# Where the spread reciprocals of the fourth pair are loaded in layer 0, and where the last pair's reciprocal is taken in layer 1

## The chip, the cores and the metric

The kernel runs on one core of one Trainium2 chip. The metric is the time of one execution on the device in microseconds (us), the median of several runs; lower is better. The core's engines are TensorE (PE, matrix products), VectorE (DVE), ScalarE (ACT), GpSimd (POOL) and SyncE (SP). SP issues nearly all transfers (DMA); ACT issues a few in layer 0. Each engine works through its own instructions in the order of the program and waits where an operand isn't there yet.

## The reference, cut to what matters

Eight images of 384 channels and 32 x 32 pixels pass through two layers. Layer 0 is attention over the 1024 pixels with 8 heads of 48 channels and a bias per pair of positions; layer 1 is attention with 6 heads of 64 channels and normalised q and k, and then a feed-forward part. What the change touches is, in both layers, the division of the attention's output by the sums of its exponentials, and what is done with the quotient:

```python
# layer 0
attn = jnp.einsum('bhnd,bhmd->bhnm', q * scale, k)
attn = attn + _relative_bias(h, w, mlp_w1, mlp_b1, mlp_w2, mlp_b2)[None]
attn = jax.nn.softmax(attn, axis=-1)
out = jnp.einsum('bhnm,bhmd->bhnd', attn, v)
out = out.transpose(0, 2, 1, 3).reshape(b, n, c)
out = out @ proj_w + proj_b
# layer 1
attn = jax.nn.softmax(jnp.einsum('bhnd,bhmd->bhnm', q, k) * scale, axis=-1)
out = jnp.einsum('bhnm,bhmd->bhnd', attn, v)
out = out.transpose(0, 2, 1, 3).reshape(B, N, C)
return out @ proj_w.T + proj_b
```

The kernel computes exp(scores) and its product with v first, takes the sums of the exponentials along as an extra row of that product, and divides afterwards.

## The kernel before, in words

**Layout.** The eight heads of layer 0 are handled as four pairs (numbers 0 to 3; the name NF0 is 3). A pair's two heads lie in the two halves of 64 partitions (S0 = 64) of a tile of 128 x 1024. A head needs only 48 of its 64 partitions, so the fourth pair's rows are also laid into the spare partitions of the other three: the output projection then has three products over the pairs in place of four. `oT` holds the attention's output of all four pairs; row 0 of each half of a pair is the sum of the exponentials.

**The boundary between two images in layer 0.** While PE finishes image b, the next image's queries and keys are projected, in six blocks n = 0 to 5 (keys and queries of the first pair, then of the second and third). A block's products come out of PE; `take` (line 677, ACT) copies the smaller part to a tile `t`; `add` (line 683, DVE) adds the larger part; `halves` splits the result: ACT makes the rounded high half `h` (line 696) and issues its stores (lines 701 and 703, tensor `halves` in memory), DVE makes the low half by subtraction (line 697), and SP issues its stores (the same two lines). The fourth pair's rows of q and k sit in the other pairs' tiles, so for the first pair the operands are put together on the chip by transfers from tile to tile (`move`, line 719): two for the queries' last operand, at once; two in `fill_q`; and eight in `fill_k`, the tiles called `h`, `l` and `km` in the profile.

**The division of a pair** (`divide`, line 947 on): two transfers bring the row of sums to memory (`sd`); `invert` reads them back in another shape and POOL raises them to the power -1 (line 961); `keep_inverse` stores the reciprocals (`rd`, line 967); `spread` loads them twice, each time broadcast over 64 partitions (`rb`, two transfers of 256 KB, line 984); `multiply` multiplies `oT` by them on POOL (line 988); for the fourth pair `spread_rows` copies its rows into the spare partitions of the other pairs' `oT` (six transfers, line 1000). Then comes the output projection of image b, `pp` (line 1011).

**What sets the order.** The order is written out by hand. `_Later.after(n, work)` puts work down for the n-th next call of `step()`, and `step()` is called at fixed places of the program, for example at the end of each `add` (line 683). The tuple `at` in `divide` holds four such numbers: the steps from the division to `keep_inverse`, from the division to `spread`, from `spread` to `multiply`, and from `multiply` to `spread_rows`. Images 0 to 6 use the tuple that the change touches for the fourth pair. After that pair's division the steps of the boundary are, in order: add of n=0, add of n=1, add of n=2, the four parts `project_v(0)` to `project_v(3)` of the values' projection, add of n=3, add of n=4, add of n=5. In the code `fill_q` follows `project_v(1)`, `fill_k` follows `project_v(2)`; each part of the projection ends with a step. The held `halves` of block n=3 come ahead of the add of n=4. All of SP's transfers are issued in this order, and a transfer that must wait holds back those behind it.

The tiles of q, k, `t` and `h` come from one pool of slots; a slot is handed on when its last reader is done.

**Layer 1.** Images 1 to 4 take the first block of the next image's q and k between the attention of image b and its output projection. `project_cut` (line 1775 on) runs the products, ACT copies one part (line 1791), and its inner function `take` evicts: DVE combines both parts (line 1800) and ACT squares the result (line 1802). With `step=False` it returns `take` to the caller in place of running it and stepping. `divide` of layer 1 (line 1996 on) puts the sums in memory and reads them back to `inv`; its `invert` takes the reciprocal on DVE (line 2024), stores it (line 2026) and loads it spread over the partitions (`rb`, two transfers, line 2033); `multiply` (line 2042, DVE) follows a step later, between the two parts of `project_out` (line 2076, `pp`).

Of the kernel before, what the change touches and what calls it, by code (L numbers as in the profile page):

```python
# [200 lines left out]
class _Weights:  # L201
# [32 lines left out]
    def take(self):  # L234
        for at, n, pm in self.sums:
            self.nc.vector.tensor_scalar_mul(self.mean[:, at : at + n], pm[:, :n], 1.0 / C)
# [39 lines left out]
def _layer0(tc, ins, x1, sums, shared, weights, beside):  # L276
# [9 lines left out]
    with ExitStack() as ctx:  # L286
# [14 lines left out]
        later = _Later()  # L301
# [25 lines left out]
        for g in range(P // QT):  # L327
            at = g * QN
# [618 lines left out]
        def divide(b, pair):  # L947


            o = oT[:, pair]  # L950
            sd = dram.tile([2, N], F32, tag="sd", name=f"sd{b}_{pair}")
            rd = dram.tile([2, N], F32, tag="rd", name=f"rd{b}_{pair}")
            mine = sums[:, b, pair]
            inv = kept.tile([P, 2 * N // P], F32, tag="inv", name=f"inv{b}_{pair}", bufs=2)
            for j in range(2):
                nc.sync.dma_start(sd[j : j + 1], oT[j * S0 : j * S0 + 1, pair])

            def invert():
                with nc.allow_non_contiguous_dma(reason="sums"):
                    nc.sync.dma_start(mine, sd.rearrange("j (p c) -> (j p) c", c=2 * N // P))  # L960
                    nc.gpsimd.tensor_tensor(  # L961
                        inv, mine, over.to_broadcast([P, 2 * N // P]), ALU.pow
                    )

            def keep_inverse():
                with nc.allow_non_contiguous_dma(reason="sums"):
                    nc.sync.dma_start(rd.rearrange("j (p c) -> (j p) c", c=2 * N // P), inv)

            if b == B - 1 or b == 0 and pair < NF0:
                invert()  # L970
                at = (2, 2 if pair == NF0 else 3, 2, 0)
            elif pair == NF0:
                invert()
                at = 2, 5, 2, 1
            else:
                later.after(1, invert)
                at = 3, 4, 2, 0
            later.after(at[0], keep_inverse)
            rb = []

            def spread():
                rb.append(kept.tile([P, N], F32, tag="rb", name=f"rb{b}_{pair}"))
                for j in range(2):
                    nc.sync.dma_start(rb[0][ts(j, S0)], rd[j].partition_broadcast(S0))
                later.after(at[2], multiply)

            def multiply():
                nc.gpsimd.tensor_mul(o, o, rb[0])  # L988
                if b == B - 1:
                    if pair < NF0:  # L990
                        for j in range(2):
                            nc.gpsimd.memset(oT[j * S0 : j * S0 + SP, pair], 0.0)
                elif pair == NF0:
                    later.after(at[3], spread_rows)

            def spread_rows():
                for c in range(NF0):
                    for j in range(2):
                        row = j * S0 + SP + c * FR
                        nc.sync.dma_start(oT[j * S0 : j * S0 + SP, c], oT[row : row + FR, pair])  # L1000

            later.after(at[1], spread)
# [70 lines left out]
        for i in range(len(parts) // 2):  # L1073
            later.after(i + (13 if i < 9 else 12), lambda: grow_turns(1))
            at = 1 + i % NF0 if i < 12 else 2 + i % 2
# [480 lines left out]
def _layer1(tc, ins, x1, out, shared, start, there, before=None, check=None):  # L1556
# [4 lines left out]
    with ExitStack() as ctx:  # L1561
# [10 lines left out]
        later = _Later()  # L1572
# [138 lines left out]
        def project_qk(b, pair, s, xt, dst, sq, step=True, middle=None):  # L1711


            pq = mm2(f"pq{b}_{pair}_{s}")
            order = [(k, h) for k in range(KC) for h in range(NH)]
            for k, h in order if middle is None else sorted(order, key=lambda kh: kh[1]):
                if middle is not None and (k, h) == (0, 1):
                    middle()
                nc.tensor.matmul(  # L1719
                    pq[:, h], wqkv[:, k, s * C + pair * P : s * C + (pair + 1) * P],  # L1720
                    xt[:, k, ts(h, HALF)], start=(k == 0), stop=(k == KC - 1),
                )

            def take():
                t = qkp.tile([P, N], F32, tag="qk", name=f"qk{b}_{pair}_{s}")
                if s == 0:
                    nc.vector.tensor_copy(t, flat2(pq))
                else:
                    nc.vector.tensor_copy(
                        t.rearrange("c (m p) -> c p m", m=MT),  # L1730
                        flat2(pq).rearrange("c (p m) -> c p m", m=MT),
                    )
                dst[pair, s] = t
                q = wtile(f"qsq{b}_{pair}_{s}")
                nc.scalar.activation(q, flat2(pq), AF.Square)
                sq[pair, s] = q

            if not step:
                return take
            take()  # L1740
            later.step()
# [37 lines left out]
        def project_cut(b, n, parts, dst, sq, step=True, middle=None, order=(2, 0, 1)):  # L1779


            pair, s = BLOCKS1[n]
            name = f"{b}_{pair}_{s}"
            ps = mm2("pg" + name), mm2("pm" + name)
            for at, i in enumerate(order):
                if middle is not None and at == 2:
                    middle()
                cuts.products(n, i, ps[i // 2], (parts.high, parts.low, parts.mixed)[i])

            q = wtile("qsq" + name)  # L1790
            nc.scalar.activation(q, flat2(ps[1]), AF.Identity, scale=-1.0 / CUT)

            def take():
                t = qkp.tile([P, N], F32, tag="qk", name="qk" + name)
                to = t if s == 0 else t.rearrange("c (m p) -> c p m", m=MT)
                of = flat2(ps[0])
                if s == 1:
                    of = of.rearrange("c (p m) -> c p m", m=MT)
                with_ = q if s == 0 else q.rearrange("c (p m) -> c p m", m=MT)
                nc.vector.scalar_tensor_tensor(to, of, 1.0 + 1.0 / CUT, with_, ALU.mult, ALU.add)  # L1800
                dst[pair, s] = t
                nc.scalar.activation(with_, to, AF.Square)
                sq[pair, s] = q

            if not step:
                return take
            take()
            later.step()
# [53 lines left out]
        def project_v(b, xt, m2, c=None, copy=nc.vector.tensor_copy):  # L1862

            pv = mm2(f"pv{b}_{m2}")
            for i in range(2):
                for k in range(KC):
                    nc.tensor.matmul(  # L1867
                        pv[:, i, 0:C],
                        xt[:, k].rearrange("c (p m) -> c m p", m=MT)[:, 2 * m2 + i],
                        wv[:, k], start=(k == 0), stop=(k == KC - 1),  # L1870
                    )
            if c is None:
                copy(v[:, 2 * m2 : 2 * m2 + 2], pv[:, :, 0:C])
            else:
                for i in range(2):
                    m = 2 * m2 + i
                    nc.vector.tensor_scalar_mul(v[:, m], pv[:, i, 0:C], c[:, 1, m : m + 1])
            later.step()
# [113 lines left out]
        def weigh_last(b, oT, done):  # L1992
            for finish in weigh(b, oT, *done) or ():
                finish()
# [328 lines left out]
        for b in range(B):  # L2323
# [65 lines left out]
            else:  # L2389
                nqk, sq, d, nkc = {}, {}, head_rows(b + 1), kc_tile(b + 1)  # L2390

                def project(n, step=True, middle=None, order=(2, 0, 1)):
                    if b == 0:
                        return project_qk(b + 1, *BLOCKS[n], ahead, nqk, sq, step, middle)
                    return project_cut(b + 1, n, parts, nqk, sq, step, middle, order)
# [4 lines left out]
                if b == 0:  # L2400
                    for i in range(2):
                        project_v(b + 1, ahead, i)
                        weigh_last(b, oT, held[i])
                    divide(b, oT, [NP1 - 1], (1, 1))
                    project_v(b + 1, ahead, 2)
                else:
                    project_v(b + 1, ahead, 0)
                    weigh_last(b, oT, held[0])
                    for k in range(1, KC):
                        parts.cut_low(k)  # L2410
                    weigh_last(b, oT, held[1])
                    divide(b, oT, [NP1 - 1], (1, 1))
                    for k in range(KC):
                        parts.mix(k)
                    project(0, order=(0, 1, 2))
                fsq, fc = [], []
                project_out(b, oT, xt, lambda m, _: fsq.append(square(f"f{b}", xt, m)), later.step)
                if b > 0:
# [14 lines left out]
                if b == 0:  # L2433
                    project(1)
                    take = project(2, step=False)
# [4 lines left out]
                    take = project(3, step=False)  # L2440
# [137 lines left out]
```

## Time and profile before

| | us |
|---|---|
| median of three runs | 2915.94 |
| lowest and highest | 2912.86, 2917.39 |
| the profiled execution, its own time | 2915.22 |
| its span (first to last instruction) | 2913.4 |
| PE busy | 2872.4 (99% of the span) |
| DVE busy | 2010.5 (69%) |
| ACT busy | 1554.4 (53%) |
| POOL busy | 492.7 (17%) |

The mean granted clock of PE over the span is 0.998 of full speed, and 86% of the chain that ended last lies on PE. Layer 0 lasts to about 1340 us; the seven boundaries between its images lie about 162 us apart, the first at some 230 us.

How to read the rows: in a row of the waits, "PE s L920 <- DMA l<-h: 10.3, 6, 1.8" says that PE, ahead of the instructions of line 920 that write `s`, waited in total 10.3 us, 6 times, 1.8 at most, for a transfer that writes `l` from `h`. "SPq" is SP's queue. In a timeline each row has the start in us from the span's start, the length, the engine, the line and operation, out<-in by the program's names, the number of instructions, and in brackets the idle time just before with what ended it. Loads of weights into PE (PEld) run beside its products.

### The profile page before, as it was taken

How to read it: one execution, taken by the hardware profiler on the slowest of the kernel's cores; microseconds unless marked ns; L12 is line 12 of the kernel's file. 1: busy time of each engine (PE TensorE's matmuls, PEld its weight loads, DVE VectorE, ACT ScalarE, POOL GpSimd, SP SyncE). 2: the span in 40 equal slices, each digit the busy share in tenths (PEclk: the TensorE clock that was granted, in tenths of full speed). 3: DMA queues.
4: the chain of work that ended last, by engine and by line, in shares of the span. 5: the costliest groups of instructions: out<-in, count | busy, mean ns of one | idle time of the engine just before them, and what ended most of it. 6: DMA issues, size and time to landing. Idle time of an engine off the chain costs nothing.

```text
span 2913.4 us, 43519 instructions
## 1 busy us (share of the span) xinstructions
PE 2872.4 (99%) x16850; PEld 1648.2 (57%) x16850; DVE 2010.5 (69%) x2041; ACT 1554.4 (53%) x1888; POOL 492.7 (17%) x318
## 2 busy tenths in 40 slices
PE   8999999999999999999999999999999999999998
PEld 3465564646464554644546647647647647655553
DVE  3886868686777768673756865865865875865756
ACT  2655636364555647362734655555555555564644
POOL 3120302121120202022102203203202202211010
PEclk9999999999999999999999999999999999999999
DMA  6657575665746474753301212112112112112111
GB/s 193 198 166 207 136 237 136 192 173 167 193 139 194 131 233 99 225 142 109 110 24 31 84 32 73 68 32 72 68 32 72 68 32 73 68 41 84 41 46 39
DMA packets 177751, 324.78 MB, mean 111 GB/s; under 512 B 75744, under 2 KB 94672, under 8 KB 176256
## 3 DMA queue, kind: packets, MB, share of 16 engines
q1 hardware_dynamic: 167552, 299.88, 36.1%
q10 hardware_dynamic: 9984, 22.02, 2.4%
q8 instruction: 137, 2.24, 0.3%
q14 instruction: 78, 0.64, 0.1%
HBM read 227.50 MB, written 80.65 MB: 106 GB/s over the span
## 4 chain that ended last, share of the span: by engine, by line
PE 86%; DMA 4%; DVE 4%; ACT 2%; issue 1%; SPq 1%; ACTq 0%; POOL 0%; DVEq 0%
PE o L893 14%; PE s L1930 11%; PE o L1979 11%; PE s L920 11%; PE y2p L2224 6%; PE pg L171 6%; PE y1p L2173 5%; PE pv L1867 4%; PE pm L171 3%; PE pp L2076 3%; PE pp L1011 3%; PE vg L776 2%; PE pq L1719 2%; PE s L824 1%; PE o L855 1%
## 5 line engine op out<-in xcount | busy, mean ns | idle before, releaser
L931 ACT ACTIVATE e<-e 128x1024 f32<-128x1024 f32 x448 | 473.9, 1058 | 324.9 <-DVE e L927 301.1
L927 DVE TENSOR_TENSOR e<-s,grow 128x1024 f32<-128x1024 f32 x448 | 517.4, 1215 | 86.6 <-PE s L920 79.8
L1941 ACT ACTIVATE e<-s,kc 128x512 f32<-128x512 f32 x768 | 464.0, 694 | 172.9 <-PE s L1930 163.3
L1930 PE MATMUL s<-qk,qk 64*64 64x512 f32 x3072 | 418.9, 592 | 1.7 <-DVE oT L1989 1.4
L1979 PE MATMUL o<-e,v 64*64 64x512 f32 x3072 | 414.5, 590 | 0.0
L893 PE MATMUL o<-e,v 128*64 128x512 f32 x1792 | 407.7, 598 | 1.3 <-DVE e L927 1.2
L1930 PEld LDWEIGHTS s<-qk,qk 64*64 64x64 f32 x3072 | 153.9, 132 | 191.9 <-issue 109.3
L1956 DVE TENSOR_TENSOR t<-t,e 128x1024 f32<-128x1024 f32 x192 | 230.9, 1221 | 45.2 <-ACT e L1941 45.0
L1979 PEld LDWEIGHTS o<-e,v 64*64 64x64 f32 x3072 | 160.6, 133 | 168.2 <-issue 141.1
L920 PE MATMUL s<-q,k 64*128 64x512 f32 x2016 | 254.0, 397 | 0.3 <-DVE oT L903 0.2
L893 PEld LDWEIGHTS o<-e,v 128*64 128x64 f32 x1792 | 120.5, 136 | 233.5 <-issue 217.2
L920 PEld LDWEIGHTS s<-q,k 64*128 64x128 f32 x2016 | 182.7, 184 | 104.2 <-DVE e L927 25.1
L961 POOL TENSOR_TENSOR inv<-sums,over 128x16 f32<-128x16 f32 x32 | 93.2, 2913 | 728.5 <-DMA sums<-sd 562.6
L2160 DVE TENSOR_REDUCE parts<-y 128x1 f32<-128x1024 f32 x75 | 89.7, 1217 | 103.2 <-ACT y L2157 102.7
L1953 DVE TENSOR_TENSOR t<-e,e 128x1024 f32<-128x1024 f32 x96 | 114.1, 1223 | 58.8 <-ACT e L1941 58.6
L1836 POOL TENSOR_TENSOR hc<-hc,rsqrt 128x32 f32<-128x32 f32 x24 | 137.9, 5747 | 2.0
L988 POOL TENSOR_TENSOR oT<-oT,rb 128x1024 f32<-128x1024 f32 x32 | 76.7, 2396 | 316.9 <-DMA rb<-rd 233.0
L1867 PE MATMUL pv<-wv,bx 128*128 128x384 f32 x384 | 128.3, 491 | 0.0
L2076 PE MATMUL pp<-oT,L_attn_proj_wT 128*128 128x512 f32 x288 | 126.3, 595 | 2.0 <-DVE oT L2042 2.0
L1011 PE MATMUL pp<-oT,wp 128*128 128x512 f32 x288 | 126.3, 596 | 1.0 <-issue 0.8
L1867 PEld LDWEIGHTS pv<-wv,bx 128*128 128x128 f32 x384 | 119.4, 314 | 9.8 <-ACT e L1941 4.1
L2173 PE MATMUL y1p<-lun,w 128*128 128x512 f32 x360 | 113.6, 396 | 2.8 <-DVE lun L2123 2.7
(242 smaller groups left out, 4256.2 us busy)
## 6 DMA issues: line engine op xcount, KB each, us to landing
rb<-rd SPq DMA_DIRECT2D x110, 256.0 KB
wc<-cut SPq DMA_DIRECT2D x42, 576.0 KB
k<-halves SPq DMA_DIRECT2D x84, 192.0 KB
wc<-there SPq DMA_DIRECT2D x25, 576.0 KB
halves<-h ACTq DMA_DIRECT2D x28, 512.0 KB
halves<-t SPq DMA_DIRECT2D x28, 512.0 KB
xn<-in_x_dram SPq DMA_DIRECT2D x24, 512.0 KB
res<-in_x_dram SPq DMA_DIRECT2D x24, 512.0 KB
```

The source lines that it names most:

```text
L171: self.nc.tensor.matmul(out[:, h], w[:, i, k], part[k][:, ts(h, HALF)], start=(k == 0 and i != 1), stop=(k == KC - 1 and i != 0),)
L893: nc.tensor.matmul(po[ts(j, S0)], v[:, BT * g + i, 2 * pair + j, :], es[i][:, ts(j, HALF)], start=(i == 0), stop=(i == BT - 1),)
L920: nc.tensor.matmul(ss[i][:, j], k[c][ts(j, S0), ts(BT * g + i, P)], q[a][ts(j, S0)], start=(m == 0), stop=(m == 2),)
L927: nc.vector.tensor_add(e.rearrange("p (j q) -> p j q", j=2), ss[i], near(2 * pair, BT * g + i, h, [GW * IW, 2]),)
L931: nc.scalar.activation(e, e, AF.Exp)
L1011: nc.tensor.matmul(pps[b, m][:, h], (wp[:, k] if k < NF0 else wl)[:, ts(m, P)], oT[:, k, ts(h, HALF)], start=(k == 0), stop=(k == (NF0 if ...
L1867: nc.tensor.matmul(pv[:, i, 0:C], xt[:, k].rearrange("c (p m) -> c m p", m=MT)[:, 2 * m2 + i], wv[:, k], start=(k == 0), stop=(k == KC - 1),)
L1930: nc.tensor.matmul(s[j][ts(c, QP), i], qk[pair, 1][rows, ts(4 * m2 + 2 * i + c, QP)], qk[pair, 0][rows, ts(h, HALF)], start=True, stop=True,)
L1941: nc.scalar.activation(e[:, ts(i, HALF)], s[j][:, i], AF.Exp, scale=kc[:, pair, j, m : m + 1])
L1956: nc.vector.tensor_add(total[j], total[j], e)
L1979: nc.tensor.matmul(po[ts(j, D1), r], v[keys, 2 * m2 + i, at : at + D1], es[j][keys, ts(i, HALF)], start=(m2 == 0 and i == 0), stop=(m2 == ...
L2173: nc.tensor.matmul(py[m][:, h], w1[:, k, ts(m, P)], un[k][i][:, ts(h, HALF)], start=(k == 0 and i == 0), stop=(k == KC - 1 and i == 1),)
```

## The change

Two places are edited. In layer 0, for the fourth pair's division of images 0 to 6, `spread` runs at the seventh step after the division in place of the fifth, and `multiply` one step after it in place of two; `spread_rows` stays one step behind `multiply`. By the list of steps above the two `rb` loads go from ahead of `fill_q` to behind `fill_k`; the multiply stands one place after the loads, and the six row transfers come after the add of n=4 where they came after the add of n=3, and so behind the stores of the low half of block n=3.

In layer 1, images 1 to 4, the products of the next image's first block are issued as before, but the step (and with it `invert`: reciprocal, store and the two loads) is called ahead of the block's eviction, where it came behind it.

```diff
@@ -971,7 +971,7 @@
                 at = (2, 2 if pair == NF0 else 3, 2, 0)
             elif pair == NF0:
                 invert()
-                at = 2, 5, 2, 1
+                at = 2, 7, 1, 1
             else:
                 later.after(1, invert)
                 at = 3, 4, 2, 0
@@ -2412,7 +2412,9 @@
                     divide(b, oT, [NP1 - 1], (1, 1))
                     for k in range(KC):
                         parts.mix(k)
-                    project(0, order=(0, 1, 2))
+                    take = project(0, step=False, order=(0, 1, 2))
+                    later.step()
+                    take()
                 fsq, fc = [], []
                 project_out(b, oT, xt, lambda m, _: fsq.append(square(f"f{b}", xt, m)), later.step)
                 if b > 0:
```

## The prediction

> **What bounds the kernel now.** I read, in this order: the page's busy times, the waits of the matrix engine (PE), then one boundary between two images of layer 0 as the timelines of PE, the vector engine (DVE) and SyncE's queue (SP) show it, and last the granted clock in all seven such boundaries.
>
> The page's first part and the first rows of PE's waits:
>
> ```profile
> PE 2872.4 (99%) x16850; PEld 1648.2 (57%) x16850; DVE 2010.5 (69%) x2041; ACT 1554.4 (53%) x1888; POOL 492.7 (17%) x318
> ```
>
> ```profile
> PE s L920 <- DMA l<-h: 10.3, 6, 1.8
> ...
> PE s L920 <- DMA oT<-oT: 1.7, 1, 1.7
> ...
> PE pp L2076 <- DVE oT L2042: 2.0, 4, 0.7
> ```
>
> PE is busy 99% of the span, so only what PE itself waits for can be gained, and anything newly late for PE is paid in full. Two of its waits belong to this change: 10.3 + 1.7 us, about 1.7 at each of the seven boundaries of layer 0, and 2.0 us in layer 1.
>
> SP's queue at the first boundary (start, length of the issue, operation):
>
> ```profile
> 214.31 2.52 SPq L984 DMA_DIRECT2D rb<-rd  x2
> 216.93 1.17 SPq L719 DMA_DIRECT2D h<-t  x2
> 218.15 1.22 SPq L719 DMA_DIRECT2D km<-h  x2
> 219.41 1.96 SPq L719 DMA_DIRECT2D km<-l  x2
> 221.97 1.14 SPq L719 DMA_DIRECT2D h<-l  x2
> 223.15 7.66 SPq L719 DMA_DIRECT2D l<-h  x2
> 230.92 5.59 SPq L1000 DMA_DIRECT2D oT<-oT  x6
> ```
>
> The row `l<-h x2` takes 7.66 us where its neighbours take 1.2. SP's waits in the same stretch say why:
>
> ```profile
> SPq L719 <- DMA halves<-h: 6.5, 1, 6.5
> ```
>
> That is a wait for a store that ScalarE (ACT) issued (line 701, the high half of block n=3), of other data. The completion semaphores recorded with each transfer explain it: the transfers of SP and ACT share eight of them in rotation, and the second `l<-h` has that of ACT's store, issued at 227.59. It is the twelfth SP transfer counted from the first `rb<-rd`. The same wait stands at all boundaries (46.5 us in total with some smaller ones).
>
> PE and DVE at that place:
>
> ```profile
> 232.57 0.49 PE L920 MATMUL s<-h,l 64*128 64x512 f32 x1 [1.70 <-DMA l<-h]
> ...
> 235.79 10.54 PE L1011 MATMUL pp<-oT,wp 128*128 128x512 f32 x24 [0.20 <-issue]
> ```
>
> ```profile
> 232.13 1.23 DVE L697 TENSOR_TENSOR t<-t,h 128x1024 f32<-128x1024 f32 x1 [2.18 <-ACT h L696]
> 233.34 1.23 DVE L927 TENSOR_TENSOR e<-s,grow 128x1024 f32<-128x1024 f32 x1
> 234.48 1.22 DVE L683 SCALAR_TENSOR_TENSOR t<-pg,t 128x1024 f32<-128x1024 f32 x1
> ```
>
> PE loses 1.7 us to the late `l`, yet what follows, `pp`, begins at 235.79, just after DVE's addition of line 683 ends (235.70) and frees its PSUM slot. So the chain of DVE, not the late fill, sets when `pp` begins. The reader should also see that `pp` reads `oT`, whose spread rows (line 1000) are issued from 230.92 on, nearly five us ahead of it.
>
> The clock, from the first score product to `pp` at the first three boundaries (PE, its loads, DVE, ACT, POOL busy, granted clock, DMA share, GB/s):
>
> ```profile
> 230.14:235.79 5.65, 3.75 (x25) 2.23 (x25) 3.65 (x4) 2.41 (x3) 0.00 (x0) 1.00 0.65 186
> 392.28:399.02 6.74, 5.03 (x25) 3.39 (x24) 4.74 (x5) 2.41 (x4) 0.00 (x0) 0.75 0.59 163
> 554.77:560.47 5.70, 3.75 (x26) 2.24 (x25) 3.68 (x4) 2.40 (x3) 0.00 (x0) 1.00 0.62 183
> ```
>
> With the same stall of 1.7 us, three of the seven boundaries (the second, fourth and sixth) are granted 0.75 to 0.80 and take 6.4 to 6.8 us in place of 5.65: 1.1 more.
>
> **The change part by part.** *Part A, layer 0.* Steps of the program move two items in SP's order. The two `rb` loads (line 984) go behind the two transfers of fill_q and the eight of fill_k; the six row transfers (line 1000) go one step back, behind the three stores of the low half of block n=3. Nothing is added or removed; the multiply on POOL stays one step behind the loads.
>
> Fills. Ten transfers that took 214.31 + 2.52 to 229 with the stall come 2.5 us earlier in the queue and occupy places 1 to 10 of the rotation, ahead of the place that stalled. They end near 222–224 instead of 230.8, and PE's 1.7 us wait goes. What is late next is the DVE chain above, so at the four boundaries with a full clock this gains 0; at the three others at most the 1.1 us of the clock. Bounds for all: 0 to 12 us (the whole waits).
>
> Loads. `rb` now holds places 11 and 12. If the compiler's rotation between the two queues keeps its places, the second `rb` takes over the semaphore and the wait of the second `l<-h`: it is issued when ACT's n=3 store has landed (230.3 at the first boundary), not at 215. What follows it then lies on the path. Loads without neighbours were issued at 300.74 and had released the multiply of POOL at 305.71; its second transfer took about 3.6 us from issue to landing. The multiply takes 2.4 (row of line 988: 2396 ns). A row transfer is 0.5–0.6 of issue and about 1.9 to landing (230.92 to 232.7–233.2), with some 0.6 between multiply and issue. From the issue of the second `rb` to the first `pp`: 3.6 + 2.4 + 0.6 + 2.4 = 9.0 us. Stalled to 230.3 this makes `pp` begin at 239.3 instead of 235.79, that is +3.5. Not stalled: issued near 224, ready by 233; no loss. Bounds: 0 to +3.5 a boundary.
>
> ACT's store. fill_q also reads tile `t` of block n=1 for the last time; it ran at 216.93–218 and now ends 2.5 us earlier. Tiles of this pool go to whoever asks in the order in which they come free. In before ACT's copy of n=3 waited 2.1 us for PE's products with the mixed operand (`ACT h L696 <- PE pm L171: 2.1`), whose tile it inherits; with `t` free earlier it inherits that and can run about 2.1 us earlier. I take this as likely (some 6 in 7): then ACT's store lands 2.1 earlier, the second `rb` goes at 228.2, and `pp` begins at 237.3–237.5: **+1.7**, not +3.5. The DVE chain, which depends on the same copies, becomes early too, so only `oT` holds PE. Bounds: 0 to 2.1.
>
> SP's other waiters: behind the stalled `rb` in the queue stand the low-half stores of n=3 (1.9 us of issue, beside the loads' flight and the multiply), the six row transfers and later stores; these land well before the next image reads them back (the first `q<-halves` reads start tens of us later), so I cost them at nothing beyond `oT`. If that cover went, ACT's copies of n=4 and n=5 would wait for these stores: 0.6 us as the row `ACT h L696 <- DMA halves<-h` has it. On POOL nothing stands behind the multiply until the next image's power (idle for 19 us before it at present).
>
> Clock. After the change PE has no `l` stall, finishes its three blocks of scores by about 233.5 and then waits for `oT` some 3 us (bounds: 0, if `oT` is in time, to 5). A wait of 1.7 us halved the clock in three of seven; I take six of seven for 3 us. A halved stretch shows 0.75 over 6.74 us, or 1.7 us of full-clock work lost, and it would fall on `pp` itself, which nothing hides: 6 x 1.7 = 10.2. Bounds: 0 to 7 x 1.7 = 12.
>
> The Trainium skill, "TensorE: Matmul & The Clock Gate", Part 1: The HAM clock gate, says that the array falls to half rate only after at least one idle window of about 3.4 us. The rows differ: here a wait of 1.7 us beside other gaps was enough in three of seven. By the page's rule an idle time of 3 us costs no clock at all, and the sum would be 10.2 us lower; I keep the rows.
>
> *Part B, layer 1, four images.* The reciprocal (0.22 us, line 2024), its store and two loads go ahead of the eviction of the next image's first block (1.93, line 1800). The eviction waits for ACT's copy in any case (`1.88 <-ACT qsq L1791`), and the sums landed 3.5 us before the reciprocal started (issued 1720.08, landed about 1721.6, reciprocal at 1725.07), so the reciprocal fits in DVE's idle time and the eviction is not delayed. `oT` is ready up to 3.4 us earlier, PE needs 0.3 to 0.7: the 2.0 us go whole. **-2.0**; bounds: -2.0 to +0.9 (the reciprocal ahead of an eviction four times, nothing gained). The SP order here (reciprocals, two loads, `wc`) stays.
>
> *Sum.* 4 x 1.7 (full-clock boundaries) + 3 x 0.6 (the others, which already paid 1.1) + 10.2 - 2.0 = +16.8 on the profiled execution's 2915.2: **2932**. That execution is 0.7 under the median of the runs shown, 2915.94, which I count as nothing: a measurement of this kernel can tell about 0.2%, 5.8 us, from no change.
>
> **The rivals.**
>
> *Faster: the second `rb` draws another semaphore (0.20).* ACT's transfers take places in the same rotation, and moving two SP transfers can shift who shares with whom. Then `rb` goes at 222–224 and `oT` is early. With ACT's copy 2.1 us earlier the DVE chain lets `pp` begin 2.1 earlier at four boundaries and 3.2 at three: 8.4 + 9.6 + 2.0 = -20, or 2895. For it: ACT's three stores of n=3 stand between SP's transfers in the rotation, and a store that slips by one place pairs with another transfer. Against: places 1 to 12 of SP keep their number, only their owners change. It decides once the second `rb` is issued before about 226.
>
> *Slower yet: the wait stays and ACT's copy does not move (0.10).* +3.5 at four, +2.4 at three, seven clock losses of 1.7, minus 2.0: 14 + 7.2 + 11.9 - 2 = +31, or 2946.
>
> *The change does nothing there (0.10).* No stall for `rb`, no earlier copy, so the DVE chain still sets `pp`: -2.0 and at most 3 x 1.1: 2910 to 2913. For it: `0.20 <-issue` shows that `pp` isn't held by the fills today.
>
> **How the numbers follow.** My forecast has 0.60; its own range is 2920 (no clock loss at most boundaries) to 2942. The two rivals below hold 0.30, the one above 0.10; the range that leaves out no more than two in ten runs from 2894 to 2946. Faster by over 0.2% is the first rival alone: 0.20. Within it, the third: 0.10. Slower: 0.60 + 0.10.
>
> **What would show it.** Right: `l<-h` issued back to back and PE's wait for it gone; a wait `halves<-h` of 4–7 us now at line 984; PE waiting for `oT<-oT` before line 1011; granted clock under 1 in the first 4 us of `pp`; line 2076 no longer waiting for line 2042. Wrong: `rb` issued without a wait; `pp` earlier after the first score product than 5.65 us; or the wait drawn by a row transfer of line 1000 instead, which would cost less as only the last pair of rows would be late.

## The result, and the profile after

The changed kernel took 2933.34 us (median; 2932.03 to 2934.56) against 2916.66 for the kernel before on the same chip: a ratio of 1.0062, 95% interval 1.005 to 1.0074. It is slower, by 0.6%. (The ratios here and below are those on record for all runs of both kernels; they differ by up to 0.0006 from the quotient of the two medians.) Its profiled execution has a span of 2930.6 us, 17.2 more than before, and a mean granted clock of 0.993 (0.998 before).

PE executes the same 16850 products in both kernels, so the start of each product in one trace can be set against its start in the other. The difference grows only in layer 0: it is 1.2 us ahead of the first boundary, 22.4 at the end of layer 0, and 17.2 at the last output projection of layer 1. From the first boundary to the end of layer 0 the change costs 21.2 us, and layer 1 gave 5.2 back.

The page's first part, and PE's waits in the changed kernel (waited for: us in total, times, longest):

```profile
PE 2878.5 (98%) x16850; PEld 1650.4 (56%) x16850; DVE 2010.0 (69%) x2041; ACT 1552.5 (53%) x1888; POOL 497.6 (17%) x318
```

```profile
PE pp L1011 <- DVE e L927: 16.3, 7, 2.5
PE s L920 <- DVE e L927: 12.5, 7, 2.7
```

PE's waits for `l<-h` (10.3 us) and for line 2042 (2.0 us) are gone. A new wait ahead of `pp` stands at all seven boundaries. SP's queue at the first boundary, and SP's wait at line 1000 from the list of its waits:

```profile
224.01 1.22 SPq L719 DMA_DIRECT2D l<-h  x2
225.27 1.23 SPq L984 DMA_DIRECT2D rb<-rd  x2
227.76 0.34 SPq L701 DMA_DIRECT2D halves<-t  x1
228.15 2.99 SPq L703 DMA_DIRECT2D halves<-t  x2
236.74 3.71 SPq L1000 DMA_DIRECT2D oT<-oT  x6
```

```profile
SPq L1000 <- DMA halves<-h: 37.6, 7, 6.0
```

The fills now go back to back and the loads follow them without a wait. The six row transfers, however, go at 236.74. What they read was ready much earlier, as POOL's timeline shows:

```profile
230.38 2.39 POOL L988 TENSOR_TENSOR oT<-oT,rb 128x1024 f32<-128x1024 f32 x1 [25.86 <-DMA rb<-rd]
```

The multiply ended at 232.8. SP held the rows back for another 4 us, for a transfer that writes `halves` from `h`. The completion semaphores recorded with the transfers (counters that tell when a transfer has landed) name it: the first row transfer has the semaphore of ACT's first store of block n=4, issued at 233.98 and landed at 236.65. At each of the seven boundaries the first row goes 0.06 to 0.09 us after that landing.

PE and DVE beside it:

```profile
236.40 0.79 PE L920 MATMUL s<-h,h 64*128 64x512 f32 x2 [2.73 <-DVE e L927]
...
239.79 12.73 PE L1011 MATMUL pp<-oT,wp 128*128 128x512 f32 x22 [1.75 <-DVE e L927]
```

```profile
233.98 1.22 DVE L697 TENSOR_TENSOR t<-t,h 128x1024 f32<-128x1024 f32 x1 [5.11 <-ACT h L696]
235.12 1.22 DVE L927 TENSOR_TENSOR e<-s,grow 128x1024 f32<-128x1024 f32 x1
236.26 1.21 DVE L683 SCALAR_TENSOR_TENSOR t<-pg,t 128x1024 f32<-128x1024 f32 x1
```

In the kernel before, `pp` began 0.1 us after the addition of line 683 at this boundary. Here that addition ends at 237.47 and `pp` begins at 239.79. The profile puts the wait down to line 927, but the second row transfer landed at 239.66, and at every boundary `pp` begins 0.13 to 0.25 us after the second row has landed. It is the rows that PE waits for; the name of an engine in a wait for several things is only that of one of them.

What this costs, from the first score product to the first `pp`, and for `pp` itself (36 products), in us at the seven boundaries:

| | to `pp`, boundary 1 to 7 | sum | `pp`, sum |
|---|---|---|---|
| before | 5.65, 6.74, 5.70, 6.77, 5.65, 6.36, 5.64 | 42.5 | 110.7 |
| after | 8.48, 7.41, 6.86, 7.08, 6.97, 8.22, 7.94 | 53.0 | 124.0 |

So 10.5 us lie ahead of `pp` and 13.3 inside it; the stretches between the boundaries were 2.5 shorter. Inside `pp` it is the clock. The first 15.7 us of `pp` at boundaries 1 and 2 (PE, its loads, DVE, ACT, POOL busy, granted clock, DMA share, GB/s), of the changed kernel and then of the kernel before:

```profile
239.79:255.48 15.69, 15.69 (x30) 6.82 (x31) 4.87 (x4) 3.02 (x3) 0.00 (x0) 0.80 0.83 256
405.80:421.50 15.70, 15.70 (x33) 6.94 (x34) 4.87 (x4) 3.03 (x3) 0.00 (x0) 0.89 0.79 250
```

```profile
235.79:251.48 15.69, 15.69 (x38) 6.80 (x38) 7.08 (x6) 4.10 (x4) 0.00 (x0) 1.00 0.77 254
399.02:414.74 15.72, 15.72 (x39) 6.83 (x38) 6.00 (x5) 4.09 (x4) 0.00 (x0) 1.00 0.83 281
```

In the same time 30 to 33 products begin in the changed kernel and 38 or 39 in the kernel before. The granted clock in this stretch is 0.80 to 0.91 at all seven boundaries of the changed kernel.

These are means. In the clock record of the traces the granted clock is either 1.00 or 0.50, and it changes only at the edges of windows of 3.41 us that follow each other at a fixed beat, whatever the kernel does. Two of these windows at the second boundary of the kernel before:

```profile
391.90:395.32 3.42, 1.71 (x11) 0.82 (x12) 1.24 (x2) 1.72 (x2) 0.00 (x0) 1.00 0.55 96
395.32:398.73 3.41, 3.41 (x19) 2.59 (x15) 3.41 (x4) 1.06 (x1) 0.00 (x0) 0.50 0.68 234
```

PE's stall of 1.7 us lies in the first of them, half of which is idle, and the second has half the clock. At the first boundary the same stall straddles an edge, with 0.6 and 1.1 us in its two windows, and the clock stays full. In the changed kernel a window with 2.0 to 2.5 us of idle time stands ahead of the fall at each boundary, and the time at half clock within `pp`, 2.95 to 6.14 us, is twice what `pp` takes above 15.69 us, to within 0.1 us.

### The profile page after: what moved, and what is told of

It is laid out like the page before. It is cut to its first block, busy times and chain, and to the rows that moved or that the text cites. A ratio compares the mean times of both kernels' runs of the same rounds, so it can differ in the third digit from the quotient of the medians.

```text
span 2930.6 us, 43516 instructions
## 1 busy us (share of the span) xinstructions
PE 2878.5 (98%) x16850; PEld 1650.4 (56%) x16850; DVE 2010.0 (69%) x2041; ACT 1552.5 (53%) x1888; POOL 497.6 (17%) x318
## 4 chain that ended last, share of the span: by engine, by line
PE 86%; DVE 5%; DMA 4%; ACT 3%; issue 2%; ACTq 1%; SPq 1%; POOL 0%; DVEq 0%
PE o L893 13%; PE s L1930 11%; PE o L1979 11%; PE s L920 10%; PE y2p L2224 6%; PE pp L1011 5%; PE y1p L2173 5%; PE pv L1867 4%; PE pp L2076 4%; PE pg L171 4%; PE pm L171 2%; PE s L824 2%; PE o L855 2%; PE pq L1719 2%; DMA halves<-h 1%
## 5 line engine op out<-in xcount | busy, mean ns | idle before, releaser
L927 DVE TENSOR_TENSOR e<-s,grow 128x1024 f32<-128x1024 f32 x448 | 517.6, 1216 | 87.8 <-PE s L920 83.0
L920 PE MATMUL s<-q,k 64*128 64x512 f32 x2016 | 253.8, 397 | 0.0
L920 PEld LDWEIGHTS s<-q,k 64*128 64x128 f32 x2016 | 182.4, 184 | 103.9 <-issue 23.5
L1011 PE MATMUL pp<-oT,wp 128*128 128x512 f32 x288 | 139.7, 648 | 16.3 <-DVE e L927 16.3
```

The lines of the kernel that those rows point to most:

```text
L920: nc.tensor.matmul(ss[i][:, j], k[c][ts(j, S0), ts(BT * g + i, P)], q[a][ts(j, S0)], start=(m == 0), stop=(m == 2),)
L927: nc.vector.tensor_add(e.rearrange("p (j q) -> p j q", j=2), ss[i], near(2 * pair, BT * g + i, h, [GW * IW, 2]),)
L1011: nc.tensor.matmul(pps[b, m][:, h], (wp[:, k] if k < NF0 else wl)[:, ts(m, P)], oT[:, k, ts(h, HALF)], start=(k == 0), stop=(k == (NF0 if ...
```

## The experiments

Two theories. **W**: the loss is the wait that the row transfers drew by sharing a completion semaphore with ACT's store; put them elsewhere and it goes. **L**: the loads are simply late now, and they share the DMA engines with ACT's stores (the third store of n=3 landed 3.8 to 5.4 us after its issue, 2.5 before), so the copy of n=4 that waits for that store is late.

**The two parts alone.** Part A alone:

```diff
-                at = 2, 5, 2, 1
+                at = 2, 7, 1, 1
```

> Part A alone (the fourth pair's tuple 2, 7, 1, 1; layer 1 as before). Theory W, a wait on a shared completion semaphore in front of the row transfers, and theory L, the loads being late and in the way of ACT's stores, both expect what layer 0 showed in the changed kernel: +21 to +23 us at the end of layer 0 against the kernel before, and with layer 1 unchanged a time of 2936 to 2940, about 3 to 5 above the changed kernel. If part B itself costs time, it would instead lie below the changed kernel's 2933.

Measured: 2935.44 us against 2918.22, ratio 1.0065 (1.005 to 1.0081). Layer 0 ended 21.8 us later than before, and with layer 1 unchanged only 1.0 came back there (20.8 later at its last projection). The time lies 0.6 us under the expected range; within the noise the whole loss is part A's.

Part B alone, the other half of the diff:

> Part B alone (reciprocal ahead of the eviction, layer 0 as before). If the 2.0 us of PE waiting for DVE's multiply are what part B removes, the time is 2.0 to 3.1 us under before (the four projections in the changed kernel were 2.6 us nearer, and 0.5 more in the products right behind them): ratio 0.9990 to 0.9993. If the rest of the 5.2 us that layer 1 gained in the changed kernel is also its doing, 0.9982. If it is only drift between executions, layer 1 between the edited projections shows either sign.

Measured: 2914.52 us, ratio 0.999 (0.9981 to 0.9999), some 2.9 us faster by the ratio and 3.7 by the medians; the interval only just leaves out no change. Within the four edited projections PE gained 0.6, 0.6, 0.8 and 1.0 us, 3.0 in all, and their wait for line 2042 is gone; between them the difference moved either way. DVE at the first of them:

```profile
1719.86 0.25 DVE L2024 RECIPROCAL inv<-inv 128x16 f32<-128x16 f32 x1 [0.20 <-DMA inv<-sd]
1721.54 1.94 DVE L1800 SCALAR_TENSOR_TENSOR qk<-pg,qsq 128x1024 f32<-128x1024 f32 x1 [1.42 <-ACT qsq L1791]
```

The reciprocal follows the sums' landing by 0.2 us, and the eviction still waits for ACT's copy, not for the reciprocal. The 5.2 us that layer 1 seemed to give back in the changed kernel were thus about 3 of the change and 2 that differ between two executions, as the 1.0 us do with part A alone.

**The row transfers a step earlier, with the loads where the change put them.**

```diff
-                    later.after(at[3], spread_rows)
+                    spread_rows()
```

> The changed kernel, with the six row transfers issued in the step of the multiply, ahead of the low-half stores of n=3 instead of behind them. In the compiled order none of them then shares a completion semaphore with an ACT store that is still to come. The loads stay where the change put them. Theory W: the rows go within 1 us of the multiply's end, pp begins when DVE's addition of n=5 ends, 5.2 to 5.8 us after the first score product in place of 6.9 to 8.5, the clock stays near 1 in pp, which takes 15.7 to 16.1 in place of 17.1 to 18.7; time 2903 to 2912, some 5 to 12 below the kernel before. Theory L: the multiply ends as late as now and the copy of n=4 waits as long for ACT's stores of n=3, so pp begins at best 1 us earlier than in the changed kernel and the clock still falls: 2925 to 2933.

Measured: 2915.63 us, ratio 0.9993 to the kernel before (0.9983 to 1.0003): nearly the whole loss is gone. SP's queue at the second boundary:

```profile
386.96 1.23 SPq L984 DMA_DIRECT2D rb<-rd  x2
394.31 4.40 SPq L1000 DMA_DIRECT2D oT<-oT  x6
398.81 0.53 SPq L701 DMA_DIRECT2D halves<-t  x1
399.38 6.83 SPq L703 DMA_DIRECT2D halves<-t  x2
```

The loads are as late as in the changed kernel, yet `pp` begins 3.5 to 6.5 us after the first score product (32.6 in sum, 10 less than before) and takes 15.69 at six of seven boundaries. That speaks for W. It is still 3.6 us above the range of W, and the trace shows why: the wait has moved on. The third low-half store of n=3 now stands where it shares a semaphore with ACT's store of n=5, which comes only after `pp` has begun, and the loads of the residuals stand behind it. From the lists of SP's and PE's waits:

```profile
SPq L703 <- DMA halves<-h: 48.0, 11, 7.0
```

```profile
PE s L920 <- DVE res L1027: 4.8, 8, 0.9
PE pp L1011 <- DMA oT<-oT: 4.6, 6, 1.1
```

About 12 us were lost again in the stretches between the boundaries, after each `pp`. The wait for `res` explains part of them; the rest I did not attribute. `pp` still begins with the second row here, 0.1 to 1.1 us after DVE's addition: that much of L is true.

**The row transfers a step later, in the kernel before.** The loads stay ahead of the fills and layer 1 is unchanged:

```diff
-                at = 2, 5, 2, 1
+                at = 2, 5, 2, 2
```

> The kernel before with one number changed: the row transfers one step later (tuple 2, 5, 2, 2); the loads stay ahead of the fills, layer 1 as before. In the compiled order the second row transfer then has the semaphore of ACT's first store of n=4. Theory W: SP waits at line 1000 for that store, pp begins 1.5 to 2.5 us later after the first score product, the clock falls in pp: 2928 to 2940 with the loads not moved at all. Theory L: rb lands as early as before and nothing is late: 2914 to 2918.

Measured: 2949.75 us, ratio 1.0114 (1.0099 to 1.013): slower than the change under study, with the loads not moved at all. `rb` had landed 17.5 us or more ahead of `pp`. The time is also 10 us above W's own range: `pp` begins 2.1 to 3.6 us later than in the kernel before where W expected 1.5 to 2.5, as that store of n=4 lands 4.5 to 5.1 us after its issue here, against 2.7 in the changed kernel. The second row transfer shares a semaphore with ACT's first store of n=4, went right after that store's landing at each boundary, and `pp` began 8.9 to 9.5 us after the first score product. SP's wait at the second boundary, and PE's row there:

```profile
SPq L1000 <- DMA halves<-h: 2.5, 1, 2.5
```

```profile
407.61 1.95 PE L1011 MATMUL pp<-oT,wp 128*128 128x512 f32 x4 [2.32 <-DMA oT<-oT]
```

L expected no change here, so it falls as the main cause; that a wait on a shared semaphore is enough is shown, its size W had too small.

**The rows from another queue.** The changed kernel, rows issued by POOL behind its multiply:

```diff
-                        nc.sync.dma_start(oT[j * S0 : j * S0 + SP, c], oT[row : row + FR, pair])
+                        nc.gpsimd.dma_start(oT[j * S0 : j * S0 + SP, c], oT[row : row + FR, pair])
```

> The changed kernel with the six row transfers issued from POOL's queue, right behind the multiply that runs there, in place of SP's. They then neither share a semaphore with ACT's stores nor hold back SP's stores and residual loads behind them (where the rows went on SP at the multiply, the wait moved on to the low-half stores, 48.0 us in total, and PE then waited 4.8 us for the residuals and pp began 0.1 to 1.1 us after DVE's addition, with the second row). If the shared semaphores are all that is left of the loss: pp begins 3.5 to 4.8 us after the first score product at most boundaries, no wait of 5 us or more of SP for halves<-h, PE not waiting for res: 2903 to 2910, below the kernel before by 0.2 to 0.5%. If the loads' own lateness is what is left (multiply ends only 4.3 to 4.6 us ahead of pp), POOL's issue of the rows is no faster than SP's and pp again waits for the second row: 2911 to 2918.

Measured: 2906.66 us, ratio 0.9965 (0.9951 to 0.9978). This beats both kernels. POOL at the second boundary:

```profile
390.15 2.40 POOL L988 TENSOR_TENSOR oT<-oT,rb 128x1024 f32<-128x1024 f32 x1 [24.37 <-DMA rb<-rd]
392.85 3.02 POOL L1000 DMA_DIRECT2D oT<-oT  x6 [0.30 <-POOL oT L988]
```

All six rows are issued within 6 us of the multiply's start at this boundary, and `pp` begins 0.1 us after DVE's addition at all seven boundaries, 4.6 to 5.8 us after the first score product (36.3 in sum); `pp` takes 15.69 at six of them. Layer 0 ends 4.7 us earlier than before. Two points of the expectation missed. `pp` begins 3.5 to 4.8 us after the first score product at only two boundaries, not at most. And SP does wait for ACT's store, now ahead of line 701,

```profile
SPq L701 <- DMA halves<-h: 44.4, 7, 7.1
```

but that is the low half of n=4, with nothing behind it that PE lacks: a wait of 44 us in total that costs nothing to be seen. The store of n=3 lands as slowly here as in the changed kernel (3.7 to 4.4 us for the third one), so what L describes is real; it only cost less than the early fills gained.

**The loads back ahead of the fills, rows still from POOL.**

```diff
-                at = 2, 7, 1, 1
+                at = 2, 5, 2, 1
```

(against the run before it).

> As the run beside it, but with the loads ahead of the fills as in the kernel before (tuple 2, 5, 2, 1; rows from POOL's queue; layer 1 as changed). The second l<-h still has the semaphore of ACT's store of n=3 or of one of its neighbours. If that keeps its wait, PE waits 1.7 us for l at the boundaries, the clock falls at two to four of them and pp begins 5.6 to 6.8 us after the first score product: 2911 to 2916. In the compiled order of this kernel the second l<-h comes eight places behind that store again, so this is the likelier. If the rows leaving SP's queue are what helps, it gains as much as the run beside it: 2903 to 2910.

Measured: 2917.4 us, ratio 1.0 (0.9991 to 1.0009), 1.4 us above the likelier range. The wait of the second `l<-h` is back, and longer:

```profile
PE s L920 <- DMA l<-h: 17.1, 7, 3.5
```

With the rows out of the way, loads behind the fills are 0.35% better than loads ahead of them. The idea of the change was sound; what undid it was the place in the queue that came with it.

**The wait that was predicted, at the loads.** In the changed kernel the three ACT stores of n=4 go to POOL's queue:

```diff
-                    for queue, x, part in ((nc.scalar, 0, up), (nc.sync, 1, down)):
+                    high = nc.gpsimd if (pair, s) == BLOCKS0[4] else nc.scalar
+                    for queue, x, part in ((high, 0, up), (nc.sync, 1, down)):
```

> The changed kernel with only the three stores of the high half of block n=4 moved from ACT's queue to POOL's (the same data to the same place; line numbers one higher). The row transfers stay on SP where the change put them. In the compiled order they then share no semaphore with a store to come, but the first rb load now has that of ACT's first store of n=3, which is the wait that the prediction described. If a wait at the loads costs what the prediction worked out: SP waits for halves<-h ahead of the loads, not ahead of the rows; the rows go within 1 us of the multiply, and pp begins 7 to 8.5 us after the first score product (store landed about 1.5 us ahead of it, second load 0.6 later, 3.6 to landing, 2.4 multiply, 0.6, 2.4 to the second row): 2925 to 2940. If only a wait at the rows can be felt, pp begins 3.5 to 5.8 us after the first score product: 2903 to 2912.

Measured: 2958.16 us, ratio 1.014 (1.0123 to 1.0157). The first `rb` load now waits for ACT's first store of n=3, at all boundaries (line numbers are one higher):

```profile
SPq L985 <- DMA halves<-h: 40.0, 7, 6.8
```

```profile
240.23 1.19 PE L1012 MATMUL pp<-oT,wp 128*128 128x512 f32 x1 [7.13 <-DMA oT<-oT]
```

PE waits 53.1 us in total for the rows, and `pp` begins 10.3 to 12.0 us after the first score product. The time is 18 us above the higher of the two expected ranges. The wait at the loads is worse here than the one at the rows, and worse than worked out: from the issue of the second load to `pp` it took 11.9 to 13.6 us, where the prediction had 9.0. The load took 4.0 to 5.0 us to land, and the second row 4.5 to 5.3 in place of 2.4, beside the stores that POOL was issuing at that time. How much of the loss is the wait and how much these slower landings, no run separates.

## Why the prediction was right, and where it was not

The forecast was 2932, the measured time 2933.34, inside both ranges. That it lies so near is in part luck. The wait came at another place than forecast, and two of the signs that the prediction names for being wrong are in the trace: `rb` issued without a wait, and a row transfer that draws it. And the sizes make up for each other: 1.9 us too little ahead of `pp` and 3.1 in the clock, against 2.5 us that the stretches between the boundaries were shorter and 3.2 more that layer 1 gave back. What held is the kind of loss: a transfer that `pp` needs waits for one of ACT's stores, and PE's idle time then costs the clock in `pp`. By its own steps:

- **Fills.** Right. They go back to back and PE's 1.7 us wait for `l` is gone at all boundaries; in the changed kernel `pp` did not begin earlier for it.
- **Loads.** This step failed. The prediction let the second `rb` take over the semaphore of ACT's store of n=3 and with it the wait. The loads went without one, at 225.27. In the compiled order ACT's three stores of n=4 now stand around the two loads, where before the first of them came between the two `l<-h`, so the partners eight places away changed. The same kind of wait fell on the first row transfer, two items later in SP's queue, for the store of n=4. The prediction had named that case as one that would cost less, "as only the last pair of rows would be late": it was the first row, and all six were late, since SP issues in order.
- **ACT's copy.** Right for n=3: at the first boundary its copy began at 225.43, 5.9 us ahead of the first score product, against 3.6 before, that is 2.3 earlier by that measure. The further claim, that DVE's chain becomes as much earlier, was not: the copy of n=4 waits for the landing of the third store of n=3, and that took 3.8 to 5.4 us in place of 2.5.
- **`pp` late.** Four times 1.7 and three times 0.6, 8.6 us, against 10.5 measured: near, but by another wait. By the prediction's own terms, 228.2 + 9.0 is 237.2, which is 1.4 later and not 1.7, so the term should have been 6.5. Where the wait does stand at the loads, in the last run above, the 9.0 were 11.9 to 13.6 and the loss is 1.4%.
- **Clock.** Six boundaries of 1.7 us, 10.2; measured 13.3, 1.1 to 3.0 at each of the seven. The mechanism was right and the size a quarter too small: at three boundaries the half clock lasted two or three windows of 3.41 us, where the prediction's 1.7 us are those of one. It also counted three blocks of scores; there are four, and the fourth waits for DVE (the row `s L920 <- DVE e L927`), which adds a second stretch of idle time. The Trainium skill, "TensorE: Matmul & The Clock Gate", Part 1: The HAM clock gate, has the clock fall after one idle window of about 3.4 us. PE's idle time between the first score product and `pp` came in two pieces of at most 2.7 us each here, and the clock fell at all seven: the rows decide. 2.0 to 2.5 us of idle time in one window of 3.41 were enough.
- **Part B.** The sign was right, the size 2.0 us against 2.9 by the ratio and 3.0 by the four projections. The waits that the profile lists count idle time alone. Products of `pp` that follow each other begin 0.43 us apart while one lasts 0.59, so a stop also costs the overlap of some 0.16: four of these make 0.6 of the missing 1.0. That share is worked out, not tested.

The rival that ended faster said that it decides once the second `rb` is issued before about 226. It was, at 225.9, at the first boundary; and yet the kernel was slower. The condition named only the first of two places where the queue could stop.

## What to carry to other kernels

A transfer can wait for one that it has nothing to do with, because both use the same completion semaphore; when transfers are moved, look eight places ahead in the compiled order for every transfer that the critical engine depends on, and not only for the one that was waiting. Moving a transfer moves the wait to another in the same queue, so ask what stands there: against the kernel before, 40.0 us of such waiting at the loads went with 1.4% more time (slower landings included), 37.6 us at the rows with 0.6% more, and 44.4 us at a store that nobody reads soon with 0.35% less. The changed kernel itself has a second such wait, 37.2 us at line 703 in total, most of it behind the rows, and it costs nothing to be seen. Short dependent transfers that end a chain may be better issued by the engine that produced their data, if its queue is free: here that turned a loss of 0.6% into a gain of 0.35%.

## What the runs showed of the hardware

- Transfers of SP and ACT complete on eight semaphores given out in turn over both queues. The wait for one is recorded in SP's queue, with the transfer or as an entry just ahead of it: the first row transfers of the changed kernel went 0.06 to 0.09 us after the earlier transfer on their semaphore had landed, though ACT had issued that one. Transfers issued by POOL did not take part in this rotation; the six rows have other semaphores there.
- The granted clock falls by windows of 3.41 us and not by single gaps. From 200 us to the end of layer 0 it fell to 0.50 43 times in the nine traces, each time after a window in which PE was idle for 1.65 us or more; no window with more than 1.81 us of idle time was followed by a full clock, and between the two either was seen. So the same stall of 1.7 us cost the clock at three of the seven boundaries of the kernel before, where it lay in one window (1.71 to 1.75 us idle), and nothing at the other four, where no window had more than 1.49.
- POOL issued six row transfers in 3.0 to 3.3 us; SP took 3.7 to 3.9 for the same six in the changed kernel, where nothing held it back between them.
